# Self-attention's softmax in another order: the joining factor between two groups' exponents, the reciprocals between two transposes

## The chip, the cores and the metric

The kernel runs on one core of one Trainium2 chip. The time is device microseconds (us) of one execution; lower is better. Each core has five engines that run beside each other, each with its own queue of instructions: TensorE (PE; its weight loads are PEld) multiplies matrices, VectorE (DVE), ScalarE (ACT) and GpSimd (POOL) work on vectors, and SyncE (SP) mostly issues DMAs. They wait for each other by semaphores.

## The reference

The program is one transformer block on a batch of 2 sequences of 1024 tokens, width 256, in float32. It has three parts, each with a layer norm ahead of it and a residual sum behind it: self-attention, cross-attention to 154 context tokens of width 192, and a gated feed-forward part. Both attentions have 16 heads of 64.

```python
h = _layernorm(x, ln1_g, ln1_b)
x = _attention(h, h, sa_wq, sa_wk, sa_wv, sa_wo, sa_bo) + x
h = _layernorm(x, ln2_g, ln2_b)
x = _attention(h, cond_emb, ca_wq, ca_wk, ca_wv, ca_wo, ca_bo) + x
h = _layernorm(x, ln3_g, ln3_b)
p = h @ ff_w1 + ff_b1
a, gate = (p[..., :D_FF], p[..., D_FF:])
h = a * jax.nn.gelu(gate, approximate=False) @ ff_w2 + ff_b2
return h + x
```

Inside an attention, the scores of a query against all keys go through a softmax before they weigh the values: `attn = softmax(q k^T * D_HEAD ** -0.5)`, `out = attn v`. The softmax takes a maximum, exponents, a sum and a division for each query.

## The kernel before, in words

**Slots.** Self-attention is cut into 16 units (2 sequences x 8 pairs of heads), and each unit into 8 slots, so there are SA = 128 slots, numbered p. Four slots (SH) make a half h: 512 queries of a unit. The loop over p in lines 908 to 930 writes the instructions of all engines in one fixed order. There is no planner: every engine's queue has its instructions in the order in which the code emits them.

**A slot's scores.** A slot has two groups, i = 0 and 1, of 64 queries for each of the two heads. `scores` (L372, matmuls at L379) fills a PSUM tile `s` of 128 partitions x 2 heads x 512 for each group. The 128 partitions hold 4 blocks of 32: block a4 has 32 queries (a4 // 2) against one half of the 1024 keys (a4 % 2). So a query's keys lie in two blocks of partitions, which are neighbours, and each block makes a softmax of its own half. There are two `s` tiles, one for each group, so the scores of the next slot's group i need the exponents of this slot's group i to have been read out.

**The softmax of a half.** VectorE takes the negative maxima of a group (L539, one for each group). ScalarE takes the exponents, two instructions a group, one for each head (L390, `exponents`), each with its sum written by a small second instruction, the accumulator read. The maxima and the sums of a slot lie together in a small tile `st`.

**Exchange and join.** Behind the exponents, `exchange` (L396) issues four small DMAs on SP (L400) that bring each block its neighbour's maxima and sums. One slot later `join` (L404) makes from both halves the joining factor and the denominator: on GpSimd two differences and a minimum (`dd`, L408 to L410), on ScalarE one exponent of 8 numbers a partition (`ee`, L412), on GpSimd a product and a sum (`zz` L414, `den` L416). `scale_groups` (L480) calls it, and returns a function `reciprocals` to be called later. That one takes the reciprocal of the denominators on VectorE (`rd`, L486) and then multiplies both groups' exponents by `rd` and `ee` on GpSimd (L490, four instructions a slot).

**Transposes and values.** `turn_groups` (L498) transposes the two scaled groups of a slot on VectorE (L504), in 32 x 32 blocks, into the tile `pT` of its half. It works on slot p - LAG, LAG being 2. When a half is complete, `self_values` (L508) weighs the values with it on TensorE (`weigh`, L426), in two parts.

**The order in a slot.** For slot p the loop emits: scores and maxima of p (`self_first`); copies left over from earlier pieces (`flush(stores)`); then `then()`, which has the four exponents of p, the join of slot p - 1, and the exchange of p; the two transposes of slot p - 2; sums of the output projection into the residual (`flush(adds)`, VectorE, L364); the reciprocals and scalings of slot p - 1 (`late()`); and one or two pieces of other work for TensorE: projections of the next unit (L296, L312), output projections (L357), or the weighted values. In some slots the norm of the next part adds small instructions to VectorE, GpSimd and ScalarE (L194 to L238), and a bias addition goes to GpSimd (L259).

After the loop, cross-attention's slots drain the last self-attention slots by `self_drain` (L574), which has the same order of join, transposes and `late()`.

Of the kernel before, what the change touches and what calls it, by code (L numbers as in the profile page):

```python
# [18 lines left out]
def tile_transformer_block(ctx: ExitStack, tc: tile.TileContext, a: dict, out: bass.AP):  # L19
    nc = tc.nc  # L20
# [16 lines left out]
    KB = 32  # L37
# [12 lines left out]
    LAG = SH // 2  # L50
# [39 lines left out]
    for n in names:  # L90
        k = w[n].shape[0] // P
# [7 lines left out]
    for n in names[:2]:  # L99
        k = w[n].shape[0] // P  # L100
# [34 lines left out]
    for n in names[2:]:  # L135
        k = w[n].shape[0] // P
# [249 lines left out]
    def exponents(u, sc, st, i):  # L386

        pr = pp_.tile([P, 2, HB], F32, tag="P", name=f"p_{u}")
        for j in range(2):
            nc.scalar.activation(  # L390
                pr[:, j, :], sc[:, j, :], AF.Exp, bias=st[:, 0, 0, i, j:j + 1],
                accum_out=st[:, 0, 1, i, j:j + 1],
            )
        return pr

    def exchange(st):  # L396

        for a4 in range(4):
            o4 = a4 ^ 1
            nc.sync.dma_start(  # L400
                out=st[a4 * KB:(a4 + 1) * KB, 1], in_=st[o4 * KB:(o4 + 1) * KB, 0]
            )
# [74 lines left out]
    SA = 2 * SH * NU  # L477
    joins, groups, halves = [], [], {}

    def scale_groups(u, st, members):  # L480

        ee, den = join(u, st)

        def reciprocals():
            rd = small.tile([P, 4], F32, tag="rd", name=f"rd_{u}")
            nc.vector.reciprocal(rd, den)  # L486
            for i, pr in enumerate(members):
                for j in range(2):
                    c = 2 * i + j
                    nc.gpsimd.tensor_scalar(  # L490
                        pr[:, j, :], pr[:, j, :], rd[:, c:c + 1], ee[:, 0, c:c + 1],
                        op0=ALU.mult, op1=ALU.mult,
                    )
                groups.append(pr)

        return reciprocals

    def turn_groups(p):  # L498
        h, g = divmod(p, SH)
        if g == 0:  # L500
            halves[h] = pt_.tile([P, 2 * NK, QH // 2], F32, tag="pT", name=f"pT_{h}")
        for i in range(2):
            c = (2 * g + i) * KB
            nc.vector.transpose(  # L504
                halves[h][:, :, c:c + KB], groups.pop(0).rearrange("p j (n k) -> p (j n) k", k=KB)
            )

    def self_values(h, part):  # L508

# [21 lines left out]
    def self_first(p):  # L531

        b, pr = units[p // (2 * SH)]
        g = p % (2 * SH)
        q, k, _ = qk["sa", b, pr]
        st = small.tile([P, 2, 2, 2, 2], F32, tag="st8", name=f"st_{p}")
        sc = [scores(f"{p}_{i}", q, k, 2 * g + i) for i in range(2)]
        for i in range(2):
            nc.vector.tensor_reduce(st[:, 0, 0, i, :], sc[i], AX.X, ALU.max, negate=True)  # L539

        def then():
            members = [exponents(f"{p}_{i}", sc[i], st, i) for i in range(2)]
            late = scale_groups(*joins.pop(0)) if joins else None
            exchange(st)
            joins.append((p, st, members))
            return late

        return then
# [25 lines left out]
    def self_drain(p):  # L574

        late = scale_groups(*joins.pop(0)) if joins else None
        if p - LAG < SA:
            turn_groups(p - LAG)
        if late:
            late()  # L580
        h, hg = divmod(p, SH)
        if hg >= LAG and h - 1 < 2 * NU:
            run(lambda: self_values(h - 1, hg - LAG))
# [278 lines left out]
    with tc.manual_schedule():  # L862
        stats, deviation, normalize, turn = norm_pieces("sa", 0, True)
        q0, q1, k0, k1, *values = self_pieces(*units[0])
        spare["bank"] = sum_tile

        def emit(*pieces):
            for piece in pieces:
                run(piece)
            flush(stores)  # L870


        warm = mm_tile("warm")

        def busy(n):
            for _ in range(n):
                nc.tensor.transpose(warm[:, :P], ident, ident)

        busy(32)
        emit(stats[0], stats[1], deviation[0])  # L880
        emit(stats[2], normalize[0], stats[3], deviation[1])
        copies = turn[0]()
        busy(10)
        emit(stats[4], normalize[1])
        copies()
        emit(stats[5], deviation[2])
        copies = turn[1]()
        busy(4)
        copies()
        emit(normalize[2], stats[6], stats[7], deviation[3])  # L890
        q_copy, copies = q0(), turn[2]()
        emit(normalize[3])
        q_copy()
        copies()
        k_copy, copies = k0(), turn[3]()
        k_copy()
        copies()
        emit(k1)
        later.append(lambda: load_pair("sa", units[1][1]))
        later.append(lambda: load_pair("sa", units[2][1]))  # L900
        later.extend(lambda t=t: load_x(nc.scalar, B - 1, t) for t in range(0, NT, 2))
        later.append(lambda: load_out("sa", nc.scalar))
        side.append((True, (), turn_rows))
        side.extend((True, (), lambda b=b: turn_context(b)) for b in range(B))
        work.extend([q1] + values)
        add_biases("sa", 0)

        for p in range(SA):
            if p % (2 * SH) == 0:
                self_beside(p // (2 * SH))  # L910
            if p == SA - SH:
                work.extend(held)
                held.clear()
            then = self_first(p)
            flush(stores)
            late = then()
            if p >= LAG:
                turn_groups(p - LAG)
            flush(adds)
            if late:  # L920
                late()
            if later:
                later.pop(0)()
            h, hg = divmod(p, SH)
            if h == 0 or hg < LAG:

                full = hg % 2 == 0 or outs and p < SA - 2 * SH
                run_work(2 if full and p < SA - 2 * SH else 1, 1, sum_tile)
            else:
                run(lambda: self_values(h - 1, hg - LAG))  # L930

        for c in range(CA):
            if c == 0:
                pTc["ring"] = pt_.tile(
                    [P, 2 * NK, QH // 2], F32, tag="pT", name="pT_ca"
                ).rearrange("p a b -> p (a b)")[:, :3 * 2 * NB * NT * KB].rearrange(
                    "p (u n j q) -> p u n j q", u=3, n=NB, j=2)
            if c == 0:
                out_pieces("sa", B - 1, 0, range(NT // 2, NT))
            if c == SH + 1:  # L940
                out_pieces("sa", B - 1, 1, range(NT))
                outs.append(lambda: load_out("ca"))
            if c == SH:
                w1, w2 = hold_gated()
            if c % len(CG) == 0:
                cross_beside(c // len(CG))
            if c % len(CG) == len(CG) - 1:
                work.extend(held)
                held.clear()
            flush(adds)  # L950
            then = cross_first(c)
            flush(stores)
            flush(lates)
            lates.append(then())
            if c <= SH:
                self_drain(SA + c)
            cross_regroup(c)
            cross_drain(c)
            cross_weigh(c)
            flush(stores)  # L960
            run_work(2, 1, n_sum=2 * (SH < c < 2 * NPAIR and c % len(CG) == 0))
            for _ in range(min(2, len(later))):
                later.pop(0)()

        for k in range(FF):
            c = CA + k
            flush(adds)
            gate_slot(k)
            flush(stores)
            flush(lates)  # L970
            if k == 3 * len(CG):
                norm_beside("ff", B - 1)
            cross_regroup(c)
            cross_drain(c)
            cross_weigh(c)
            flush(stores)
            if k == 0:
                out_pieces("ca", B - 1, 0, range(NT - 2 * TF, NT))
            if k == len(CG) + 2:
                out_pieces("ca", B - 1, 1, range(NT))  # L980
            if k > len(CG) + 2:
                for _ in range(min(2, len(gated) - 1)):
                    run(sum_slot)
                flush(stores)
            run_work(2, 1)
            if later:
                later.pop(0)()
        while gated:
            run(sum_slot)
            flush(stores)  # L990
# [32 lines left out]
```

## Time and profile before

| what | value |
|---|---|
| median of 3 runs | 1173.76 us (1172.14 to 1174.32) |
| the profiled execution: time | 1171.99 us |
| its span, first to last instruction | 1170.1 us |
| granted TensorE clock | 0.997 |
| self-attention, first maxima to last exponent | 18.6 to 728.6 us |
| TensorE busy | 1142.5 us (98%) |
| VectorE busy | 830.1 us (71%) |
| GpSimd busy | 667.5 us (57%) |
| ScalarE busy | 644.1 us (55%) |

| operation | instructions | mean ns of one |
|---|---|---|
| exponents, L390 ACT | 512 | 686 |
| their accumulator reads, L390 ACT | 512 | 202 |
| scaling, L490 POOL | 512 | 767 |
| maxima, L539 DVE | 256 | 1219 |
| transposes, L504 DVE | 256 | 1219 |
| joining factor ee, L412 ACT | 128 | 214 |
| reciprocal rd, L486 DVE | 128 | 177 |
| exchange, L400 on SP | 512 DMAs of 1 KB | 588 to issue (median) |

Busy time is an average over the whole span, and TensorE's is modelled, so a high share alone doesn't say that TensorE sets the pace at each place. An operation's mean is the time that its engine reports; operations of one engine overlap by about a tenth of a microsecond, so the distance between two starts is a little less than the duration. L with a number is the line in the code. A landing is the completion of a DMA.

### The profile page before, as it was taken

What the parts mean: (1) busy time and instruction counts of PE and PEld (TensorE: products, weight loads), DVE (VectorE), ACT (ScalarE), POOL (GpSimd) and SP (SyncE); (2) the same over time, 40 slices, a digit from 0 to 9 for tenths busy, and PEclk for the clock granted to TensorE, in tenths of its full rate; (3) what the DMA queues carried; (4) which work ended last, traced back from release to release, by engine and by line L of the source; (5) the groups of instructions that cost most, each with busy time, mean ns of one, the idle gap of its engine ahead of it and who ended that gap; (6) DMA issues with size and microseconds to landing.
All of it is one profiled execution on the core that took longest, in us unless ns stands there. A gap on an engine that the chain in (4) does not pass through costs nothing.

```text
span 1170.1 us, 31736 instructions
## 1 busy us (share of the span) xinstructions
PE 1142.5 (98%) x11931; PEld 672.0 (57%) x11931; DVE 830.1 (71%) x1170; ACT 644.1 (55%) x2055; POOL 667.5 (57%) x1563
## 2 busy tenths in 40 slices
PE   9999999999999999999999998999999999999998
PEld 6434444545545545545545443665556567888887
DVE  4888998898888898898989887547555664232222
ACT  5656676665666666566666755447655572041111
POOL 1778777877767777777777787436644453030000
PEclk9999999999999999999999998999999999999999
DMA  2411011101101101101101100166444433000000
GB/s 82 109 26 34 12 25 34 21 21 34 21 16 34 21 16 34 21 16 34 21 16 21 27 20 7 52 167 157 111 103 99 102 80 73 1 19 10 18 10 18
DMA packets 87018, 51.06 MB, mean 44 GB/s; under 512 B 30742, under 2 KB 77650, under 8 KB 86866
## 3 DMA queue, kind: packets, MB, share of 16 engines
q1 hardware_dynamic: 83650, 46.42, 17.6%
q10 hardware_dynamic: 3216, 2.62, 0.7%
q8 instruction: 94, 1.54, 0.5%
q14 instruction: 58, 0.48, 0.1%
HBM read 19.52 MB, written 2.10 MB: 18 GB/s over the span
## 4 chain that ended last, share of the span: by engine, by line
PE 78%; ACT 7%; POOL 6%; DVE 3%; issue 3%; DMA 2%; SPq 1%; DVEq 0%; ACTq 0%; POOLq 0%
PE po L426 15%; PE s L379 15%; PE pa L818 9%; PE py_sa L357 5%; PE py_ca L357 5%; PE pf L841 5%; ACT p L390 4%; PE pq_ca L296 4%; PE poc L730 4%; PE pv_sa L312 4%; PE pk_sa L296 3%; POOL p L490 3%; PE pq_sa L296 3%; PE sc L654 3%; DMA st<-st 2%
## 5 line engine op out<-in xcount | busy, mean ns | idle before, releaser
L390 ACT ACTIVATE p<-s,st 128x512 f32<-128x512 f32 x512 | 345.1, 686 | 218.7 <-DVE st L539 207.8
L490 POOL TENSOR_SCALAR p<-p,rd,ee 128x512 f32<-128x512 f32 x512 | 385.6, 767 | 43.9 <-DVE rd L486 43.3
L539 DVE TENSOR_REDUCE st<-s 128x2 f32<-128x1024 f32 x256 | 301.4, 1219 | 44.8 <-PE s L379 36.9
L504 DVE STREAM_TRANSPOSE pT<-p 128x1024 f32<-128x1024 f32 x256 | 302.4, 1219 | 0.5 <-POOL p L490 0.4
L379 PE MATMUL s<-k_sa,q_sa 64*32 64x512 f32 x4096 | 256.7, 601 | 19.1 <-ACT p L390 18.0
L426 PE MATMUL po<-pT,v_sa 64*64 64x256 f32 x4096 | 236.1, 380 | 1.2 <-DVE pT L504 1.2
L426 PEld LDWEIGHTS po<-pT,v_sa 64*64 64x64 f32 x4096 | 150.8, 133 | 110.4 <-issue 39.4
L681 POOL TENSOR_SCALAR p<-p,rden 128x154 f32<-128x154 f32 x256 | 96.8, 398 | 119.8 <-DVE rden L678 118.6
L379 PEld LDWEIGHTS s<-k_sa,q_sa 64*32 64x32 f32 x4096 | 59.6, 106 | 151.5 <-ACT p L390 64.2
L670 ACT ACTIVATE p<-sc,neg 128x154 f32<-128x154 f32 x256 | 96.0, 394 | 88.6 <-DVE rden L678 84.4
L818 PE MATMUL pa<-hT_ln,wf 128*128 128x256 f32 x512 | 121.0, 379 | 0.0
L827 DVE SCALAR_TENSOR_TENSOR u<-pa,cols,gate 128x256 f32<-128x256 f32 x64 | 31.0, 484 | 124.1 <-ACT gate L824 124.1
L824 ACT ACTIVATE gate<-pa,cols 128x256 f32<-128x256 f32 x64 | 30.3, 474 | 152.1 <-PE pa L818 152.1
L818 PEld LDWEIGHTS pa<-hT_ln,wf 128*128 128x128 f32 x512 | 96.8, 190 | 13.7 <-issue 0.8
L390 ACT ACTIVATION_READ_ACCUMULATOR p<-s,st 128x1 f32 x512 | 103.6, 202 | 0.0
L659 DVE TENSOR_REDUCE neg<-sc 128x6 f32<-128x924 f32 (+1 forms) x48 | 48.6, 1013 | 48.4 <-PE sc L654 48.4
L414 POOL TENSOR_TENSOR zz<-ee,st 128x8 f32<-128x8 f32 x128 | 25.9, 202 | 81.6 <-ACT ee L412 81.6
L312 PEld LDWEIGHTS pv_sa<-sa_wv,hT_ln 128*128 128x128 f32 x512 | 59.3, 192 | 16.3 <-issue 13.8
L841 PE MATMUL pf<-wf,u 128*128 128x256 f32 x256 | 65.0, 379 | 0.2 <-DVE u L827 0.2
L312 PE MATMUL pv_sa<-sa_wv,hT_ln 128*128 128x128 f32 x512 | 62.4, 278 | 0.0
L296 PE MATMUL pk_sa<-hT_ln,sa_wk 128*128 128x512 f32 (+1 forms) x132 | 60.8, 596 | 0.2 <-ACT q_sa L305 0.2
L357 PE MATMUL py_ca<-ca_wo,o_ca 128*128 128x256 f32 x256 | 60.8, 384 | 0.3 <-ACT hT_ln L238 0.3
(73 smaller groups left out, 1230.1 us busy)
## 6 DMA issues: line engine op xcount, KB each, us to landing
wf<-pT_ca SPq DMA_DIRECT2D x128, 128.0 KB
st<-st SPq DMA_DIRECT2D x512, 1.0 KB
v_sa<-v_sa SPq DMA_DIRECT2D x64, 128.0 KB
wf<-in_L_xattn_ff_w_dram SPq DMA_DIRECT2D x12, 256.0 KB
sa_wq<-in_L_xattn_sa_wq_dram SPq DMA_DIRECT2D x16, 128.0 KB
sa_wk<-in_L_xattn_sa_wk_dram SPq DMA_DIRECT2D x16, 128.0 KB
sa_wv<-in_L_xattn_sa_wv_dram SPq DMA_DIRECT2D x16, 128.0 KB
ca_wq<-in_L_xattn_ca_wq_dram SPq DMA_DIRECT2D x16, 128.0 KB
```

What stands on the lines that cost most here:

```text
L296: nc.tensor.matmul(pq[:, own], lhsT=wt[:, c, :], rhs=h[:, c, n * HB + own.start:n * HB + own.stop], start=(c == 0), stop=(c == NC - 1),)
L312: nc.tensor.matmul(pv[:, i * P:(i + 1) * P], lhsT=h[:, c, (n * GT + i) * P:(n * GT + i + 1) * P], rhs=wt[:, c, :], start=(c == 0), stop=(c ...
L357: nc.tensor.matmul(py[:, :D], lhsT=o[:, i, t * P:(t + 1) * P], rhs=wo[kind][:, half * HP + i, :], start=(i == 0), stop=(i == HP - 1),)
L379: nc.tensor.matmul(sc[a4 * KB:(a4 + 1) * KB, j, :], lhsT=q[r, c:c + KB], rhs=k[r, h * HB:(h + 1) * HB], start=True, stop=True, tile_positi ...
L390: nc.scalar.activation(pr[:, j, :], sc[:, j, :], AF.Exp, bias=st[:, 0, 0, i, j:j + 1], accum_out=st[:, 0, 1, i, j:j + 1],)
L426: nc.tensor.matmul(po[a2][j * DH:(j + 1) * DH, :QH // 2], lhsT=v[r, t, e, j * DH:(j + 1) * DH], rhs=pT[r, j * NK + n, :], start=(t == 0 an ...
L490: nc.gpsimd.tensor_scalar(pr[:, j, :], pr[:, j, :], rd[:, c:c + 1], ee[:, 0, c:c + 1], op0=ALU.mult, op1=ALU.mult,)
L504: nc.vector.transpose(halves[h][:, :, c:c + KB], groups.pop(0).rearrange("p j (n k) -> p (j n) k", k=KB))
L539: nc.vector.tensor_reduce(st[:, 0, 0, i, :], sc[i], AX.X, ALU.max, negate=True)
L681: nc.gpsimd.tensor_scalar(pr_[:, j, i, :T], pr_[:, j, i, :T], rden[:, j, i:i + 1], 1.0, op0=ALU.mult, op1=ALU.mult,)
L818: nc.tensor.matmul(pa[:, half, :TF * P], lhsT=w1[:, c, half * DF + f * P:half * DF + (f + 1) * P], rhs=h[:, c, t0 * P:(t0 + TF) * P], star ...
L841: nc.tensor.matmul(sums[blk][i][:, :D], lhsT=sums[blk, "u"][:, f, i * P:(i + 1) * P], rhs=w2[:, f, :], start=(f == 0), stop=(f == NF - 1),)
```

## The change

Three places in the order differ. Nothing is computed differently.

1. In `then()`, the first group's exponents of slot p are emitted, then the join of slot p - 1 (through `scale_groups`), then the second group's exponents, then the exchange. Before, the join stood behind both groups.
2. `turn_groups` is split. `turn_group(p, i)` transposes one group, and `turn_groups(p, between)` emits group 0's transpose, then calls `between`, then emits group 1's.
3. The loop and `self_drain` hand `late`, the reciprocals and scalings, to `turn_groups` as `between`. Before, it was called after both transposes, and in the loop after `flush(adds)` too.

```diff
-    def turn_groups(p):
+    def turn_group(p, i):
         h, g = divmod(p, SH)
-        if g == 0:
+        if g == 0 and i == 0:
             halves[h] = pt_.tile([P, 2 * NK, QH // 2], F32, tag="pT", name=f"pT_{h}")
-        for i in range(2):
-            c = (2 * g + i) * KB
-            nc.vector.transpose(
-                halves[h][:, :, c:c + KB], groups.pop(0).rearrange("p j (n k) -> p (j n) k", k=KB)
-            )
+        c = (2 * g + i) * KB
+        nc.vector.transpose(
+            halves[h][:, :, c:c + KB], groups.pop(0).rearrange("p j (n k) -> p (j n) k", k=KB)
+        )
+
+    def turn_groups(p, between):
+
+        if 0 <= p < SA:
+            turn_group(p, 0)
+        if between:
+            between()
+        if 0 <= p < SA:
+            turn_group(p, 1)
...
         def then():
-            members = [exponents(f"{p}_{i}", sc[i], st, i) for i in range(2)]
+            members = [exponents(f"{p}_0", sc[0], st, 0)]
             late = scale_groups(*joins.pop(0)) if joins else None
+            members.append(exponents(f"{p}_1", sc[1], st, 1))
             exchange(st)
             joins.append((p, st, members))
             return late
...
     def self_drain(p):
 
         late = scale_groups(*joins.pop(0)) if joins else None
-        if p - LAG < SA:
-            turn_groups(p - LAG)
-        if late:
-            late()
+        turn_groups(p - LAG, late)
...
             late = then()
-            if p >= LAG:
-                turn_groups(p - LAG)
+            turn_groups(p - LAG, late)
             flush(adds)
-            if late:
-                late()
             if later:
                 later.pop(0)()
```

## The prediction

> **What bounds the kernel now.** I read the page first, then the busy time by stage, then one slot of the timeline, then the waits. The page says 98% busy for TensorE. Cut into stages, the self-attention part (18.6 to 724.6 us, 128 slots) is not uniform. Columns: stretch, length, then busy time of PE, PEld, DVE, ACT, POOL, clock, DMA share, GB/s.
>
> ```profile
> 63.40:213.00 149.60, 140.35 (x1845) 65.69 (x1851) 133.85 (x154) 100.69 (x292) 118.91 (x260) 1.00 0.11 24
> 213.00:576.00 363.00, 363.00 (x4760) 188.13 (x4745) 322.41 (x350) 224.84 (x677) 266.18 (x599) 1.00 0.12 24
> 576.00:724.60 148.60, 140.73 (x1871) 67.74 (x1869) 131.26 (x153) 97.19 (x286) 113.83 (x255) 0.98 0.10 21
> 724.60:1170.00 445.40, 438.87 (x2892) 317.52 (x2876) 200.61 (x450) 183.72 (x705) 140.05 (x381) 1.00 0.28 67
> ```
>
> In the middle, TensorE never pauses, and a slot lasts what its matmuls last: in the chain of work, 1.88 us of scores (L379) and some 3.62 us of weighted values or projections, 5.50 together. On both sides it pauses 9.3 and 7.9 us in all. So an exponent, a transpose or a join costs nothing while it keeps ahead of a 5.5 us beat; the question is whether the new order can hold that beat.
>
> One slot's lines, from the timeline (start us, length us, engine, line, operation):
>
> ```profile
> 476.64 0.69 ACT L390 ACTIVATE p<-s,st 128x512 f32<-128x512 f32 x1
> 477.21 0.21 ACT L390 ACTIVATION_READ_ACCUMULATOR p<-s,st 128x1 f32 x1
> 477.31 0.22 ACT L412 ACTIVATE ee<-dd 128x8 f32<-128x8 f32 x1
> 477.49 2.83 SPq L400 DMA_DIRECT2D st<-st  x4
> ...
> 478.40 3.01 POOL L490 TENSOR_SCALAR p<-p,rd,ee 128x512 f32<-128x512 f32 x4 [0.32 <-DVE rd L486]
> ...
> 481.38 0.20 ACT L390 ACTIVATION_READ_ACCUMULATOR p<-s,st 128x1 f32 x1
> 481.47 0.69 ACT L390 ACTIVATE p<-s,st 128x512 f32<-128x512 f32 x1
> 481.69 0.20 POOL L408 TENSOR_TENSOR dd<-st 128x4 f32<-128x4 f32 x1 [0.28 <-DMA st<-st]
> 481.84 0.20 POOL L409 TENSOR_TENSOR dd<-st 128x4 f32<-128x4 f32 x1
> 482.04 0.20 ACT L390 ACTIVATION_READ_ACCUMULATOR p<-s,st 128x1 f32 x1
> 482.13 0.25 POOL L410 TENSOR_SCALAR dd<-dd 128x8 f32<-128x8 f32 x1
> ```
>
> Slot 82's fourth exponent ends at 477.42. Its maxima and sums go out by four DMAs, and only at 481.69 can GpSimd begin the join (dd), which is done at 482.38. By then ScalarE has finished the first group of slot 83 (481.58) and is in its second (from 481.47). Today ee of slot 82 stands behind all four exponents of slot 83, so this lateness is harmless. The waits agree (in total us, times, longest):
>
> ```profile
> POOL zz L414 <- ACT ee L412: 81.6, 128, 2.6
> POOL dd L408 <- DMA st<-st: 39.0, 38, 13.9
> ACT ee L412 <- POOL dd L410: 18.0, 39, 2.0
> ```
>
> GpSimd waits for ee in every slot, which is surely what one sees first; ee itself waits for its data in only 39.
>
> **What the Trainium skill says.** "Perfetto Trace Analysis", Per-engine timelines: ScalarE, VectorE and GpSimd take their instructions strictly first in, first out. The trace agrees: all 128 ee stand behind their slot's four exponents, in the order of the code. "DMA: Bandwidth & Descriptors", Anatomy of one DMA: some 2 us of fixed cost whatever the size, mostly completion. Here the 1 KB DMA lands 1.74 us (median) after its issue, as four issues of 0.6 us each stand in line. "Runtime: NRT & Kernel Launch", Instruction fetch mechanics: instructions come in 16 KiB blocks over a DMA queue. The trace has 94 such packets (queue 8, 1.54 MB), about 1.09 us each, 72 of them in this stage.
>
> **The change, part by part.** No instruction or DMA is added or removed; three places in the order differ.
>
> (a) On ScalarE, ee of slot p-1 moves ahead of the second group's exponents of slot p. On GpSimd (dd, dd, minimum, zz, den, four scalings) and on SP nothing changes place. The exchange of slot p still goes out behind its fourth exponent. But what now stands behind ee in its queue are the very exponents whose sums the next exchange waits for, so a loop closes within one slot. All links are over the 128 slots of the trace:
> - last exponent's end to the landing of the last of its four DMAs: least 3.52, median 3.65, mean 4.00, most 6.17 us (0.06 to the first issue, 1.82 from first to fourth issue, 1.74 to land);
> - landing to dd, where dd waits for it: 0.16;
> - dd, dd, minimum: 0.70;
> - minimum to ee: 0.03;
> - ee to the next exponent: 0.10 (as from 477.21 to 477.31);
> - two exponents with their accumulator reads: 1.45.
>
> The sum is 2.44 plus the landing: 5.96 at least, 6.09 at the median, 6.44 in the mean. Before, the same links went around with four exponents in two slots (1.35 us more, 7.8 in 11), so they never bound. Now every slot needs 6.4 us where the matmuls need 5.5. For ee not to wait, in a slot of 5.5 us, the landing would have to come by 5.5 + 2.60 (first group's end after the slot's first maximum) - 4.05 (last exponent's end) - 0.88 (0.16 + 0.70 + 0.03) = 3.17 us. The fastest of 128 is 3.52.
>
> The mean applies, not the median, because the loop has no slack that could absorb a late landing. 57 exchanges have an instruction packet in flight and take 4.38 us in the mean, the other 71 take 3.70. With slots of 6.44 in place of 5.56 and the same number of packets, the hit share falls from 0.445 to about 0.38, so I take 3.70 + 0.38 x 0.69 = 3.96, and a loop of 6.40. From slot 0's last exponent (22.72) to slot 127's (728.65) it is 705.9 us now; 127 x 6.40 = 812.8, or +107.
>
> (b) On VectorE, the reciprocal of slot p-1 moves from behind both transposes and the adds to between the transposes. It waits for den there, and behind it stand the second transpose, the adds of the output projection, and the next slot's maxima. Loop: reciprocal to transpose 0.10, transpose 1.16 to the next start, maximum to exponent 1.26, first group 1.34, ee to den 0.77, den to reciprocal 0.03: 4.66, and 5.5 with two adds of 0.41. That is under 6.09, so it hides behind loop (a). If (a) weren't there, it would nearly fill the 5.5 beat. The weighted values read the second transpose. The reciprocal comes 0.80 after ee, 0.75 before the slot's last exponent ends; the transpose ends some 0.6 after that end, and the next weighted values start 1.3 after it (0.24 to wake TensorE, 1.09 for half the scores). So 0.7 us covers it, and I cost it at nothing.
>
> (c) GpSimd's scalings start sooner after ee. Its loop is 0.77 + 0.03 + 0.28 + 3.01 + 0.70 + 0.03 = 4.82, and 5.55 with a bias addition (0.73). With the norm's var and rstd (0.19 + 0.71) it is 6.45: about eight slots in this stage, some 0.3 us each, and slot 126 keeps its 8.0. I add 3 us. TensorE's own: 0.24 wake, 1.09 half the scores, 3.63, 1.09 is 6.05, just under the loop.
>
> Cross-attention and feed-forward come after and stay at 441 us from slot 127's last exponent on. Sum on the profiled execution: 1171.99 + 107 + 3 = 1282. The median of the runs is 1.8 us above it, which is no more than their scatter; I predict 1282.
>
> **The rivals.**
> 1. Late landings hide after all (packets fall outside the window of the exchange): 6.09 per slot, 127 x 6.09 = 773, +67 to +80: 1240 to 1255. For it: packets follow the instruction streams and may shift in phase. Against: 57 of 72 fall in the window now.
> 2. A second loop takes hold (through the reciprocal, second transpose, adds and next maxima, which 0.9 us of slack guards): a further 0.5 us a slot, +64: 1310 to 1350. For it: VectorE is 89% busy in the middle stage. Against: 5.5 against 6.4.
> 3. Faster: the join's data is there when ee comes up, zz no longer waits (81.6 us today), the scalings start earlier, and half of TensorE's pauses in the outer stages (1.6 + 9.3 + 7.9) go: -9, 1163. This decides from landings within 3.17 us; none is. It would need the exchange to be faster than any seen.
> 4. The move does nothing, since TensorE at 5.5 a slot hides all of it: 1174. Against it is the loop's 5.96 at its very least.
>
> **How the numbers follow.** The loop at its mean (1255 to 1310) 0.78, rival 1 0.09, rival 2 0.08, rival 3 0.03, rival 4 0.02. The time is the likeliest's, 1282. Leaving out at most 2 in 10, the range goes from 1245 to 1310; the two ends are the median landing, with part of its upper band, and the first slots of rival 2. A measurement can't tell changes under 0.2% (2.3 us) from none; faster 0.03, same 0.02, slower 0.95.
>
> **What would show it.** ee's wait for dd goes from 18.0 us in 39 to most of 128, 80 to 160 us. dd waits for the exchange in most slots, not 38. zz's wait for ee falls to its latency, 0.32 x 128 = 41. Slots are 6.2 to 6.6 us in all of the stage. TensorE's scores wait for exponents in all of it (64.2 and 18.0 us today), with pauses of 0.5 us and more in the middle stage, which has none. The stage after slot 127 keeps its length. It is wrong if ee doesn't wait, if exchanges land in under 3.2 us, or if slots stay at 5.5 with ee waiting: then the exponents' loop has slack that I have not seen.

## The result, and the profile after

The changed kernel takes 1288.62 us (median; 1287.27 to 1290.86) against 1173.44 us before: a ratio of 1.0986, 95% interval 1.097 to 1.1003. Forecast was 1282, with 1245 to 1310 as range. The profiled execution took 1287.32 us, its span is 1285.4 us.

Busy time by stage of the changed kernel (stretch, length, then busy time of PE, PEld, DVE, ACT, POOL, clock, DMA share, GB/s). The stretches are shifted with the longer stage:

```profile
74.00:240.00 166.00, 141.78 (x1777) 62.65 (x1780) 125.55 (x148) 97.60 (x280) 113.89 (x251) 0.97 0.10 21
240.00:640.00 400.00, 360.06 (x4531) 172.07 (x4522) 297.74 (x328) 215.97 (x636) 253.03 (x565) 0.99 0.10 20
640.00:838.00 198.00, 169.73 (x2138) 78.40 (x2144) 150.28 (x178) 113.81 (x333) 131.43 (x294) 0.97 0.09 18
838.00:1285.00 447.00, 439.37 (x2908) 317.78 (x2892) 200.54 (x451) 183.41 (x706) 139.69 (x381) 1.00 0.28 67
```

TensorE, which never paused in the middle stage before, now pauses 40 us in 400 there, and every other engine is less busy too. All engines have more idle time and the program is longer, which points to latencies that go around in a loop; the experiments below test it. Slot 127's last exponent ends at 844.6 us (728.6 before); from there to the end it is 440.8 us, as before (441.5). All of the loss lies in self-attention's slots.

The waits of the changed kernel (total us, times, longest):

```profile
PEld s L379 <- ACT p L390: 217.1, 140, 4.3
DVE rd L486 <- POOL den L416: 199.3, 128, 3.3
POOL dd L408 <- DMA st<-st: 195.6, 123, 13.9
ACT ee L412 <- POOL dd L410: 193.6, 126, 3.3
...
POOL zz L414 <- ACT ee L412: 42.2, 128, 1.0
```

ee waited 18.0 us in 39 slots before; now 193.6 us in 126. dd's wait for the exchange went from 39.0 to 195.6. The wait that one sees first before, zz for ee, did shrink as the new order makes it, from 81.6 to 42.2; that brought nothing. One turn of the loop, from the timeline of the changed kernel (start us, length us; lines of other work are left out):

```profile
500.98 0.20 ACT L390 ACTIVATION_READ_ACCUMULATOR p<-s,st 128x1 f32 x1
...
501.24 9.91 SPq L400 DMA_DIRECT2D st<-st  x8
...
504.14 0.20 ACT L390 ACTIVATION_READ_ACCUMULATOR p<-s,st 128x1 f32 x1
...
506.41 0.20 POOL L408 TENSOR_TENSOR dd<-st 128x4 f32<-128x4 f32 x1 [2.68 <-DMA st<-st]
506.56 0.20 POOL L409 TENSOR_TENSOR dd<-st 128x4 f32<-128x4 f32 x1
506.85 0.25 POOL L410 TENSOR_SCALAR dd<-dd 128x8 f32<-128x8 f32 x1
507.13 0.21 ACT L412 ACTIVATE ee<-dd 128x8 f32<-128x8 f32 x1 [2.80 <-POOL dd L410]
507.25 0.67 ACT L390 ACTIVATE p<-s,st 128x512 f32<-128x512 f32 x1
...
508.48 0.20 ACT L390 ACTIVATION_READ_ACCUMULATOR p<-s,st 128x1 f32 x1
```

A slot's last exponent ends at 501.18. The first group of the next slot is done at 504.34, and then ScalarE stands still for 2.80 us, with its second group's exponents behind ee, until the exchange of the slot before has come in. The second group ends at 508.68, 7.50 us after 501.18, in a slot whose exchange was late. And the page's chain of work (the work that ended last, followed back from the last instruction) has moved to the exchange. In the kernel before it was:

```profile
PE 78%; ACT 7%; POOL 6%; DVE 3%; issue 3%; DMA 2%; SPq 1%; DVEq 0%; ACTq 0%; POOLq 0%
```

In the changed kernel it is:

```profile
PE 32%; DMA 20%; SPq 18%; ACT 15%; POOL 7%; issue 5%; DVE 2%; ACTq 0%; POOLq 0%; DVEq 0%
DMA st<-st 19%; SPq L400 18%; ACT p L390 13%; PE pa L824 9%; PE py_ca L357 4%; PE pf L847 4%; PE pq_ca L296 4%; PE poc L736 4%; PE sc L660 3%; POOL dd L410 2%; POOL dd L408 2%; POOL dd L409 2%; PE py_sa L357 2%; ACT ee L412 1%; PE pv_ca L624 1%
```

### The profile page after: what moved, and what is told of

It is laid out like the page before. It is cut to its first block, busy times and chain, and to the rows that moved or that the text cites. A ratio compares the mean times of both kernels' runs of the same rounds, so it can differ in the third digit from the quotient of the medians.

```text
span 1285.4 us, 31613 instructions
## 1 busy us (share of the span) xinstructions
PE 1174.5 (91%) x11931; PEld 664.9 (52%) x11931; DVE 819.4 (64%) x1170; ACT 649.8 (51%) x2055; POOL 670.4 (52%) x1563
## 4 chain that ended last, share of the span: by engine, by line
PE 32%; DMA 20%; SPq 18%; ACT 15%; POOL 7%; issue 5%; DVE 2%; ACTq 0%; POOLq 0%; DVEq 0%
DMA st<-st 19%; SPq L400 18%; ACT p L390 13%; PE pa L824 9%; PE py_ca L357 4%; PE pf L847 4%; PE pq_ca L296 4%; PE poc L736 4%; PE sc L660 3%; POOL dd L410 2%; POOL dd L408 2%; POOL dd L409 2%; PE py_sa L357 2%; ACT ee L412 1%; PE pv_ca L624 1%
## 5 line engine op out<-in xcount | busy, mean ns | idle before, releaser
L379 PE MATMUL s<-k_sa,q_sa 64*32 64x512 f32 x4096 | 279.7, 609 | 101.3 <-ACT p L390 99.8
L503 DVE STREAM_TRANSPOSE pT<-p 128x1024 f32<-128x1024 f32 x256 | 312.3, 1220 | 0.0
L547 DVE TENSOR_REDUCE st<-s 128x2 f32<-128x1024 f32 x256 | 298.3, 1202 | 16.4 <-PE s L379 15.1
L426 PE MATMUL po<-pT,v_sa 64*64 64x256 f32 x4096 | 244.0, 389 | 1.6 <-DVE pT L503 1.6
L426 PEld LDWEIGHTS po<-pT,v_sa 64*64 64x64 f32 x4096 | 154.4, 137 | 118.3 <-issue 36.5
L379 PEld LDWEIGHTS s<-k_sa,q_sa 64*32 64x32 f32 x4096 | 48.5, 105 | 265.8 <-ACT p L390 217.1
L486 DVE RECIPROCAL rd<-den 128x4 f32<-128x4 f32 x128 | 22.7, 178 | 199.3 <-POOL den L416 199.3
L408 POOL TENSOR_TENSOR dd<-st 128x4 f32<-128x4 f32 x128 | 25.4, 199 | 196.0 <-DMA st<-st 195.6
L412 ACT ACTIVATE ee<-dd 128x8 f32<-128x8 f32 x128 | 26.7, 209 | 193.6 <-POOL dd L410 193.6
L390 ACT ACTIVATION_READ_ACCUMULATOR p<-s,st 128x1 f32 x512 | 100.3, 196 | 0.0
```

The costliest lines, as they stand in the source:

```text
L379: nc.tensor.matmul(sc[a4 * KB:(a4 + 1) * KB, j, :], lhsT=q[r, c:c + KB], rhs=k[r, h * HB:(h + 1) * HB], start=True, stop=True, tile_positi ...
L390: nc.scalar.activation(pr[:, j, :], sc[:, j, :], AF.Exp, bias=st[:, 0, 0, i, j:j + 1], accum_out=st[:, 0, 1, i, j:j + 1],)
L426: nc.tensor.matmul(po[a2][j * DH:(j + 1) * DH, :QH // 2], lhsT=v[r, t, e, j * DH:(j + 1) * DH], rhs=pT[r, j * NK + n, :], start=(t == 0 an ...
L503: nc.vector.transpose(halves[h][:, :, c:c + KB], groups.pop(0).rearrange("p j (n k) -> p (j n) k", k=KB))
```

## The experiments

My theory: ee, put ahead of the second group, closes a loop within a slot (last exponent, exchange, dd, ee, second group, last exponent), and the exchange's latency is the bulk of it. The rival: VectorE's queue, where the reciprocal now stands waiting between the transposes.

**One part alone.** The first kernel moves only the join:

```diff
-            members = [exponents(f"{p}_{i}", sc[i], st, i) for i in range(2)]
+            members = [exponents(f"{p}_0", sc[0], st, 0)]
             late = scale_groups(*joins.pop(0)) if joins else None
+            members.append(exponents(f"{p}_1", sc[1], st, 1))
```

> The kernel before, with the join between the two groups' exponents alone; the reciprocals stay behind both transposes and the adds. Theory (a loop within one slot: last exponent, exchange, dd, ee, second group's exponents): the loop doesn't pass the reciprocal, so nearly the whole loss is here: 1280 to 1292 us, slots of 6.4 to 6.5, ee waiting for dd in over 120 of 128 slots. Rival (the loss comes from VectorE, where the reciprocal waits between the transposes and holds the second transpose and the maxima): 1174 to 1190 us.

Measured: 1287.49 us, ratio 1.0966 (1.0945 to 1.0988), the same as the whole change. The mean from one slot's last exponent to the next is 6.47 us in both. This part by itself brings the whole loss. Its waits:

```profile
ACT ee L412 <- POOL dd L410: 286.3, 127, 4.6
...
DVE rd L486 <- POOL den L416: 107.6, 116, 3.3
```

ee waits 93 us longer here than in the whole change, with the same time for the program. A wait inside a loop is what the other links leave over: here the maxima aren't held up by the reciprocal (the exponents wait 75.7 us for them, 160.0 in the whole change), so the first group is ready sooner and ee waits longer. Its size is no measure of the loss.

The second kernel moves only the reciprocals, with the change's `turn_groups` and `then()` as before:

> The kernel before, with the reciprocals between the two transposes alone; ee stays behind all four exponents. Theory: the within-slot loop through the exchange is gone (ee waits as seldom as before, about 18 us in all), but another closes on VectorE: ee to rd 0.80, rd to second transpose 0.10, transpose 1.16, maxima to exponent 1.26, four exponents 2.77, 6.1 a slot, and more with adds: 1245 to 1270 us; the part is slower alone too, and with ee moved ahead that loop is 4.7 to 5.5 and hidden. Rival 1 (all of the loss of the whole change is this part): 1285 or more. Rival 2 (a wait of rd between transposes is hidden, since the transposes are two slots old): 1170 to 1180 us.

Measured: 1248.06 us, ratio 1.0631 (1.0613 to 1.0648); 6.15 us from slot to slot. So this part is slow as well when it is alone, by another loop, and ee hardly waits for dd (2.8 us in 6). From its timeline:

```profile
500.33 0.18 DVE L486 RECIPROCAL rd<-den 128x4 f32<-128x4 f32 x1 [1.24 <-POOL den L416]
500.43 1.22 DVE L503 STREAM_TRANSPOSE pT<-p 128x1024 f32<-128x1024 f32 x1
...
501.57 0.72 DVE L364 TENSOR_TENSOR x<-py_sa,x 128x256 f32<-128x256 f32 x2
502.21 2.34 DVE L547 TENSOR_REDUCE st<-s 128x2 f32<-128x1024 f32 x2
503.45 0.69 ACT L390 ACTIVATE p<-s,st 128x512 f32<-128x512 f32 x1 [3.71 <-DVE st L547]
...
506.12 0.21 ACT L412 ACTIVATE ee<-dd 128x8 f32<-128x8 f32 x1
...
506.93 0.18 DVE L486 RECIPROCAL rd<-den 128x4 f32<-128x4 f32 x1 [1.23 <-POOL den L416]
```

The reciprocal holds the second transpose, the adds and the maxima; the exponents wait 3.71 us for the maxima; ee comes behind all four of them, and the next reciprocal behind ee: 6.60 us around here, with two adds in it. So the losses of the two parts don't add up: both are loops, and the longer one sets the slot. With ee moved ahead as well, the second loop loses two exponents and falls under the first.

**More of the suspected latency.** Two DMAs of 512 bytes ahead of each exchange, in the changed kernel and in the one before. They wait for the slot's last exponent as the exchange does, and nobody reads what they bring.

```diff
+    unused = one.tile([P, 2, 2, 2], F32, tag="unused", name="unused")
     def exchange(st):
+        for n in range(2):
+            nc.sync.dma_start(out=unused[:KB, n], in_=st[:KB, 0, 1])
         for a4 in range(4):
```

> The changed kernel, with two more DMAs of 512 bytes ahead of each exchange on SP, which read the slot's sums and so wait for its last exponent; nobody reads what they bring. They put off the exchange by two issues, some 1.24 us. Theory: the exchange is a link of the loop that sets every slot, so all of it is paid: 127 x 1.24 = 157 us more than the changed kernel's 1288, 1430 to 1460 us. Rival (the changed kernel's pace is set elsewhere, by VectorE or TensorE, and the exchange has slack): less than 1320 us.

Measured: 1444.38 us, ratio to the kernel before 1.2312 (1.2283 to 1.2341). That is 155.8 us more than the changed kernel's 1288.62, where 157 was worked out. Last exponent to landing rose from 4.03 to 5.25 us in the mean, and the slot from 6.47 to 7.68. All of the delay is paid in every slot: the exchange is a link of the loop that sets the pace.

> The kernel before, with the same two DMAs ahead of each exchange. Theory: there the loop has two slots (11 us) for a sum of 4.00 + 1.24 + 0.16 + 0.70 + 0.03 + 0.10 + 2.77 = 9.0 us, so the same 1.24 us is hidden but for the latest landings and the slots at either end of the stage: 1174 to 1195 us. Rival (a late exchange is paid in any order): 1300 us or more.

Measured: 1228.82 us, ratio 1.0467 (1.0449 to 1.0485). The same DMAs cost 55 us here, a third of what they cost in the changed kernel, but far more than the 0 to 21 that I had allowed. Two things were missing in my sum. First, SP's queue: with six issues, and value exchanges in between, the landing came 5.52 us after the last exponent, not 5.24. Second, a path: from ee on through zz and den to the reciprocal, behind which the next slot's maxima stand on VectorE (the reciprocal's wait for den rose from 36.5 to 110.2 us). With it the loop over two slots is landing + 0.16 + 0.70 + 0.03 + 0.80 + 0.28 + 1.26 + 2.77 = 11.5, over the 11.0 that TensorE needs, so this delay isn't hidden. For the kernel before it is 10.0: by this sum the exchange had 1.0 us of slack in two slots, not the 3.2 that the loop through ee alone leaves (7.8 in 11.0).

> The kernel before, with one DMA of 512 bytes ahead of each exchange in place of the two of the run before, which cost 55 us where next to nothing was expected. Theory, mended by that run: the kernel before has a loop over two slots which goes on from ee through zz and den to the reciprocal, behind which the next maxima stand on VectorE: landing + 0.16 + 0.70 + 0.03 + 0.80 (ee to rd) + 0.28 (rd to maxima) + 1.26 + 2.77. With the landing at 4.00 in the mean that is 10.0 us of the 11.0 that two slots last; with two DMAs ahead (landing 5.52 measured) 11.5 to 11.8. With one it should be 4.65 to 4.75 of landing and 10.7, still under 11.0, so that only late landings are paid: 1176 to 1195 us. Rival (what was paid is the length of SP's queue or any delay of the exchange, in proportion): half of 55 us, 1200 us or more.

Measured: 1195.19 us, ratio 1.0194 (1.0177 to 1.0211), at the upper edge of the theory's range. The first DMA puts the landing off by 0.80 us in the mean and costs some 23 us, the second by 0.72 and costs 32. That is more than in proportion, as a limit would have it, but the difference between the two theories is small. In the traces the time over two slots is within 0.35 us of that sum for 17% of the slots without a DMA ahead, 49% with one and 63% with two. Taking each slot's own landing, and 11.0 where the sum is less, gives 11.0, 11.2 and 11.6 us over two slots in the mean; the traces have 11.1, 11.5 and 12.0. So the mended path accounts for a little more than half of the rise, and the rest stays open.

**Less of the suspected latency.** Four copies on ScalarE behind the fourth exponent do the exchange, 32 partitions x 8 numbers each, in place of the four DMAs:

```diff
-            nc.sync.dma_start(
-                out=st[a4 * KB:(a4 + 1) * KB, 1], in_=st[o4 * KB:(o4 + 1) * KB, 0]
-            )
+            nc.scalar.copy(
+                st[a4 * KB:(a4 + 1) * KB, 1], st[o4 * KB:(o4 + 1) * KB, 0]
+            )
```

In the changed kernel:

> The changed kernel, with the exchange done by four small copies on ScalarE (32 partitions x 8 each), behind the fourth exponent, in place of the four DMAs. Estimate for the copies from the spacing of small ScalarE instructions here: 4 x 0.10 to 0.2 us, so exchange to landing falls from 4.0 to under 1 us and the within-slot loop from 6.5 to about 3.5. Theory (the exchange's latency is what the loss is made of): ee waits for dd hardly at all, the middle slots are TensorE's 5.5 us again, and the pauses of the outer slots shrink, since zz no longer waits behind four exponents: 1150 to 1174 us, at or below the kernel before. Rival (the order itself is slow, by VectorE's in-order wait for the reciprocal or by ee splitting the exponents): 1200 us or more.

Measured: 1162.86 us (1162.62 to 1163.0), ratio to the kernel before 0.9911 (0.9896 to 0.9926). This beats both kernels. With the changed order kept and most of the latency gone, the whole loss turns into a gain, so the rival falls: in the changed order as a whole, neither ee between the groups nor the reciprocal between the transposes costs anything by itself. A slot of it, and its waits:

```profile
503.01 0.20 ACT L390 ACTIVATION_READ_ACCUMULATOR p<-s,st 128x1 f32 x1
503.10 0.20 ACT L412 ACTIVATE ee<-dd 128x8 f32<-128x8 f32 x1
503.20 0.68 ACT L390 ACTIVATE p<-s,st 128x512 f32<-128x512 f32 x1
...
504.43 0.21 ACT L390 ACTIVATION_READ_ACCUMULATOR p<-s,st 128x1 f32 x1
504.67 0.81 ACT L400 COPY st<-st 32x8 f32<-32x8 f32 x4
```

```profile
POOL zz L414 <- ACT ee L412: 107.6, 128, 2.9
...
POOL p L490 <- DVE rd L486: 40.5, 127, 0.4
...
ACT ee L412 <- POOL dd L410: 7.7, 10, 1.3
```

From the last exponent's end the copies are done after 0.85 us in the mean, where the DMAs took 4.0. ee follows the first group with no pause, and TensorE is busy for all of the middle stage again:

```profile
213.00:576.00 363.00, 363.00 (x4710) 189.30 (x4695) 316.20 (x351) 278.23 (x937) 264.05 (x598) 1.00 0.10 24
```

The gain is in the slots on either side, where TensorE had pauses: slot 127's last exponent ends at 720.5 us, 8 us sooner than before.

In the kernel before:

> The kernel before, with the same four copies on ScalarE in place of the DMAs. Theory: there the exchange was hidden (e4 has shown how far), so little is to be won: 1165 to 1178 us. It tells whether a gain of the changed kernel with copies comes from the copies alone, or from the order that they make possible.

Measured: 1166.14 us (1165.64 to 1167.14), ratio 0.9941 (0.9928 to 0.9953). Most of the gain comes from the copies, some 7 of 10 us; the new order adds 3.3 us once the exchange is fast.

With the join alone moved:

> The join between the groups alone (reciprocals behind both transposes), with the copies. Theory: no loop above 5.5 us either; it differs from the whole change with copies only in where the reciprocal stands, and GpSimd's scalings start up to one transpose (1.16 us) later: 1155 to 1178 us, between the kernel before with copies and the changed kernel with copies.

Measured: 1174.16 us, ratio 1.0011 (1.0005 to 1.0018): slower than both, where I had it between them. The waits:

```profile
POOL p L490 <- DVE rd L486: 108.8, 125, 1.7
...
ACT ee L412 <- POOL dd L410: 54.9, 93, 1.7
```

ee waits again, this time not for the exchange: den is ready early, but its reciprocal stands behind both transposes and the adds, so the scalings start late (108.8 us of waiting against 40.5), and GpSimd comes late to the next dd, for which ee now has the second group's exponents behind it. The trace bears this out: in 86 of the 128 slots dd begins within 0.2 us of the last scaling's end and ee follows it at once; with the reciprocal moved too it is 11. With the fast exchange, moving the join forward needs the reciprocal moved as well. I had priced the later start of the scalings and not followed it to the next dd.

## Why the prediction was right, by its own steps

- **What bounds the kernel before.** TensorE at 5.50 us a slot in the middle stage: right; the copies' kernels come back to it.
- **(a) The loop.** Right, link by link. In the changed kernel the landing is 4.03 us in the mean, then 0.16, 0.69, 0.04, 0.12 and 1.43: 6.47, where 6.40 was forecast. From slot 0's last exponent to slot 127's it is 821.6 us; 812.8 was forecast. The join alone, the two DMAs ahead and the copies show that this is the cause.
- **The mis-sized term.** The slot came out 0.07 us longer than forecast, all of it in the landing (4.03 against 3.96). I took the share of exchanges that meet an instruction packet from 0.445 down to 0.38, because slots grow longer. It was 61 of 128, 0.48, and these took 4.45 us against 3.65 for the rest. The plain mean of the trace before would have been nearer. That packets are what delays the exchange stays a coincidence in the records, a strong one (49 of the 50 landings over 4.0 us have one in flight); no run took the packets away.
- **(b) VectorE's loop, hidden behind (a).** Right: without this part (the join alone) the time is the same. I said that it would nearly fill the 5.5 us beat without (a); with the join moved and the exchange fast it fits, as TensorE's 5.5 us come back. With ee left where it was, four exponents are in this loop instead of two, and it takes 6.15 us a slot.
- **(c) The extra 3 us for norm slots and slot 126.** Not seen: the eight slots with the norm's var and rstd take 6.30 us in the mean, no longer than the 6.47 of all, and slot 126, 8.4 us before, takes 6.6. Only the first eight slots are longer, 6.78. So the 3 us were a wrong term that made up for part of the landing's.
- **The stage behind.** 440.8 us, 441 forecast.
- **Rival 3, faster.** Its condition, landings within 3.17 us, was not met by any exchange of the changed kernel either (least 3.56). Given that condition, by the copies, the time comes out as it said: 1163 forecast, 1162.86 measured. That is luck. Of its links, zz's wait didn't go away: it is 107.6 us with the copies, more than the 81.6 before. And two thirds of the gain come with the copies in the old order too, where the rival's reasons don't hold.
- **Signs.** ee's wait was to be 80 to 160 us and is 193.6, too low a figure. zz's wait (41 forecast) is 42.2, and dd waits in 123 slots. TensorE's scores wait 217.1 and 99.8 us for exponents (64.2 and 18.0 before). Slots of 6.2 to 6.6 us hold for the means of long stretches (6.44 to 6.46 after the first eight), not for single slots: 17% of them lie in that range.
- **The fixed cost of a DMA.** The section of "DMA: Bandwidth & Descriptors" that the prediction names describes DMAs issued by GpSimd; those of the exchange are issued on SP. The argument doesn't rest on its 2 us but on the measured links, 1.74 us from issue to landing and 4.0 for the four together.

One step failed without a bearing on the forecast, the account of the kernel before: its "7.8 in 11" left out the path from ee to the next maxima, which the DMAs ahead then showed.

## What to carry to other kernels

Before moving an instruction forward in an engine's queue, ask what then stands behind it, and whether its data comes, however many engines and DMAs away, from that same work one step earlier: then a loop closes. Where its links add up to more than the step takes anyway, the difference is paid in every step, and late transfers with it: here the mean landing counted, not the median. A wait's total doesn't tell the loss; the sum of the links against the beat does. And when such an order is wanted, shorten the longest link first: here four transfers of 1 KB between partitions were worth doing on an engine.

## What the runs showed of the hardware

- Four DMAs of 1 KB from SBUF to SBUF on one queue take 3.5 us at the least from the last producer's end to the landing of the last, most of it standing in line (1.82 us for the issues) and completion (1.74). Four copies of the same data on ScalarE, across groups of 32 partitions, took 0.81 us.
- The granted TensorE clock fell with TensorE's pauses: 0.997 before, 0.987 after, 0.955 with two DMAs ahead of the changed kernel's exchange, 0.998 with the copies. The mean score matmul went from 601 to 609 ns. "TensorE: Matmul & The Clock Gate" of the Trainium skill (Part 1: The HAM clock gate) puts the throttled state behind an idle window of about 3.4 us. These traces show it after shorter pauses. Ahead of the program's end the changed kernel has eight stretches at half clock, of 3.4 or 6.8 us. For six of them the longest pause of TensorE in the 12 us ahead was 2.0 to 2.7 us, going by the modelled ends of its matmuls; for the two stretches of the kernel before it was 2.3 and 2.4. The loop's links add up to the whole slot (6.47 us), so I count no time for the clock.
